# A graph layer's merged stage: items kept in flight over the ends of turns, and a group's last steps moved to the next round

## The chip, the cores and the metric

The kernel runs on one core of a Trainium2 chip. The metric is device time in microseconds, from the median of three runs; smaller is better. A profile of one further execution gives the times of single instructions. TensorE (PE) does the matrix products, VectorE (DVE), ScalarE (ACT) and GpSimd (POOL) the elementwise work, and SyncE (SP) only issues transfers. Each engine has its own stream of instructions, and they wait for one another by semaphores.

## What is computed

Two layers of a graph network on 32768 nodes of 256 features, with 524288 edges. The first layer normalizes each row, applies relu, and runs attention with 8 heads inside blocks of 128 nodes; the second sends messages along the edges in both directions and gates the result:

```python
h = jnp.maximum(_layernorm(x, axis=-1), 0.0)
x = x + _L0_gnn_ref(h, ...)               # attention inside blocks of 128 nodes
h = jnp.maximum(_layernorm(x, axis=-1), 0.0)
# inside the second layer, after a batch norm of h over all nodes:
a_in  = segment_sum(feat_in[src] * iw[:, None], dst, num_segments=N)
a_out = segment_sum(feat_out[dst] * ow[:, None], src, num_segments=N)
# a gate (sigmoid, tanh) of a_in, a_out and h gives the new h
x = x + h
```

The edges come sorted by `dst`, and most of them end at nodes with low numbers.

## The kernel before, in words

The kernel sorts the edges by block of `dst`, builds tables, and then runs a merged stage in which two kinds of work share the engines. After it come the sums over edges and the gates, which the change doesn't touch.

**Groups.** A group is 4 blocks of 128 nodes; there are 64. `project` (layer norm, queries, keys, values) and `attend` (scores, softmax, output, residual sum `x1g`, second layer norm `h1g`, its transpose `h1T`, stores of all three to memory, statistics) each return a table from step number to work. Block `b` of `attend` begins at step `B = 1 + 15 * b`; the last steps of a group reach step 74. Most intermediate values in PSUM have one buffer per name (`mx`, `sc`, `pt`, `mm`).

**Items.** An item is 128 edges with a common block of `dst`. Its steps are: `fetch` (SP loads the block's 128 rows of `h1` from memory into `hb`), `spread_lanes` (TensorE, `bc`, for four items at once), `select` (VectorE: `selT` for four items, the one-hot `oh` for each), `rank` (TensorE: three products into `R`, which counts how many edges of each source block came before), `product` (TensorE: `mp`, the rows of the edges), `place` (VectorE: `jk`, which reads the place out of `R`, and for four items `pi`), `scale` (ScalarE: `msg`) and `scatter` (GpSimd: four indirect transfers for four items). Step `t` of a turn fetches item `t`, ranks and multiplies item `t - 12`, and scales and scatters item `t - 13`.

**Rounds and turns.** A round is 64 items together with one group (`attend` of a group and `project` of the next). There are 68 rounds, in three phases (22, 23, 23). `turns` writes the instructions of a loop body: turns of 4 rounds, whose loop lets engines be in neighbouring quarters of the body (`quarter` marks the borders, and the point 14 steps into a quarter where an engine waits for its work of the quarter before); then turns of 1 round, whose loop ends in a barrier of all engines; then turns of 1 round without groups. Within a turn the items of a round begin while those of the round before are still under way, and the last steps of a group fall among the first steps of the next round. At a turn's end both are worked off: a turn of `n` items has `n + 13` steps.

**The order.** Inside a body it is written out by hand: for each step `t`, first the tables of the next round (`window` at step 10, `derive` from step 24), then the items' steps, then what the groups have put at this step, blocks in order. TensorE, VectorE, ScalarE and SP execute in this order. Steps are counted here from a round's beginning.

**The lead.** A fetched row must have been stored by a group of an earlier round. The number of groups that run alone ahead of the first round (`lead`) is worked out from the tables before the stage begins. With these inputs it is 1: the load of `xg`, one for each `project`, stands at 952.5 us and 1032.9 us before the first round begins at 1073.5 us, and 63 rounds have a group.

Of the kernel before, what the change touches and what calls it, by code (L numbers as in the profile page):

```python
# [499 lines left out]
def gnn_kernel(ctx, tc, x, src, dst, edge_attr, edge_type, w_in_e, w_out_e,  # L500
# [133 lines left out]
    lead = cpool.tile([P, 1], F32, name="lead")  # L634
    UG = 4
# [3 lines left out]
    with tc.tile_pool(name="ld", bufs=1) as lp:  # L639
        need = lp.tile([P, 1], F32, name="need")  # L640
        nc.vector.memset(need, 1.0)
        before = lp.tile([P, 1], F32, name="before")
        nc.vector.memset(before, 0.0)
        for k in range(K):
# [8 lines left out]
            nc.vector.tensor_sub(v, v, r)  # L653
            nc.vector.tensor_scalar(v, v, before[0:CI], None, op0=ALU.subtract)
# [32 lines left out]
    with ExitStack() as c1:  # L687
# [56 lines left out]
        def project(g, qT, kbd):  # L744
# [69 lines left out]
            for b, t in ((0, 47), (2, 67)):  # L814
                ps = {}
                for i in range(2):
                    @at(t + i)
                    def _(b=b, i=i, ps=ps):
                        if i == 0:
                            ps["v"] = a_ps.tile([P, 2, D], F32, name="mx")  # L820
                        for k in range(KC):
                            nc.tensor.matmul(ps["v"][:, i], hT[:, k, (b + i) * P:(b + i + 1) * P], wv[:, k],
                                             start=(k == 0), stop=(k == KC - 1))

                @at(t + 2)
                def _(b=b, ps=ps):
                    nc.scalar.copy(vg[:, b:b + 2, :, 0:DH], ps["v"].rearrange("p b (h d) -> p b h d", d=DH))

            @at(67)
# [5 lines left out]
        def attend(g, qT, kbd, bias=None):  # L835

            todo, at = steps_of()
            for b in range(GB):
                B = 1 + 15 * b
# [73 lines left out]
                if b < GB - 2:  # L913
                    continue

                bs = slice(0, b + 1) if b < GB - 1 else slice(b, b + 1)

                @at(B + 21)
                def _(bs=bs):
                    std(1, bs)  # L920

                @at(B + 22)
                def _(bs=bs):
                    nc.vector.reciprocal(rstd[1][:, bs], rstd[1][:, bs])
                    nc.vector.scalar_tensor_tensor(nmr[:, bs], mv[1][:, bs, 0], -1.0, rstd[1][:, bs],
                                                   op0=ALU.mult, op1=ALU.mult)

                for n, u in enumerate(range(bs.start, bs.stop)):
                    h = {}

                    @at(B + 23 + 3 * n)
                    def _(u=u):
                        nc.scalar.activation(h1g[:, u], x1g[:, u], AF.Relu, bias=nmr[:, u:u + 1], scale=rstd[1][:, u:u + 1])

                    @at(B + 25 + 3 * n)
                    def _(u=u, h=h):
                        h["tp"] = transposed("mx", h1g[:, u])

                    @at(B + 26 + 3 * n)
                    def _(u=u, h=h):  # L940
                        nc.scalar.copy(h1T[:, :, u * P:(u + 1) * P], h["tp"])

            @at(B + 21)
            def _():
                nc.scalar.dma_start(x1_g[g], x1g)

            @at(B + 24)
            def _():
                nc.sync.dma_start(h1_g[g], h1g)

            @at(B + 28)
# [14 lines left out]
        with tc.tile_pool(name="a_k", bufs=1) as kp:  # L966
# [3 lines left out]
            emit(attend(0, qTs[0], kbds[0], bias))  # L970
        lead_n = planned(4 * K, 1, NG)
        with tc.For_i(1, lead_n, 1) as it:
            emit(project(it, qTs[0], kbds[0]))
            emit(attend(it, qTs[0], kbds[0]))
        emit(project(lead_n.with_bounds(min_val=0, max_val=NG - 1), qTs[0], kbds[0]))
# [3 lines left out]
        LEAD = 12  # L979
        fp = c1.enter_context(tc.tile_pool(name="p_f", bufs=1))  # L980
        wp = c1.enter_context(tc.tile_pool(name="p_w", bufs=2))
        sp = c1.enter_context(tc.tile_pool(name="p_s", bufs=2))
        op = c1.enter_context(tc.tile_pool(name="p_o", bufs=7))
        ip = c1.enter_context(tc.tile_pool(name="p_i", bufs=NM))
        hp = c1.enter_context(tc.tile_pool(name="p_h", bufs=14))
# [14 lines left out]
        w0n = fp.tile([CI, 1], F32, name="w0n")  # L1000
        msgs = []
# [5 lines left out]
        def spread(k, lo, hi):  # L1007
# [57 lines left out]
            def begin(c):  # L1065
                for name, t, nxt in (("row", [1, CI], rown), ("dlb", [CI, T1], dlbn), ("ed", [P, 4, CI], edn)):
                    c[name] = wp.tile(t, nxt.dtype, name=f"{name}c")
                    nc.vector.tensor_copy(c[name], nxt)

            def fetch(i, q, c, turn):  # L1070
                if q % 4 == 0:
                    c["at"] = numbers(c["row"][:, q:q + 4], [N - P] * 4)
                hb = turn["hb", i] = hp.tile([P, D], F32, name="hb")
                nc.sync.dma_start(hb, h1_d[ds(c["at"][q % 4], P)])

            def spread_lanes(i, q, c, turn):
                if q % 4 == 0:
                    bc = turn["bc"] = bp.tile([P, 4, T1], F32, name="bc")
                    for j in range(4):
                        nc.tensor.matmul(bc[:, j], cn["pick"][:, q + j], c["dlb"], start=True, stop=True)  # L1080

            def select(i, q, c, turn):
                if q % 4 == 0:
                    sel = turn["sel", i // 4] = sp.tile([P, 4, T1], F32, name="selT")
                    nc.vector.tensor_scalar(sel, turn["bc"], cn["lane"], None, op0=ALU.is_equal)
                oh = turn["oh", i] = op.tile([P, NB], BF16, name="oh")
                nc.vector.tensor_scalar(oh, cn["iota1"], c["ed"][:, 0, q:q + 1], None, op0=ALU.is_equal)  # L1087

            def product(i, q, c, turn):
                if i % 2 == 0:  # L1090
                    turn["mp"] = pp.tile([P, 2, D], F32, name="mp")
                mp = turn["mp", i] = turn["mp"][:, i % 2]
                nc.tensor.matmul(mp, turn["sel", i // 4][:, q % 4], turn.pop(("hb", i)), start=True, stop=True)  # L1093

            def add(what, of, to, turn):
                oh = turn["oh", of]
                nc.tensor.matmul(R[:, to % 2], cn[what], oh, start=False, stop=False, skip_group_check=True)  # L1097

            def rank(i, q, c, turn):

                if i:
                    add("ones_b", i - 1, i, turn)
                if i > 1:
                    add("triu", i - 2, i, turn)
                add("tri", i, i, turn)

            def scale(i, q, c, turn):
                msg = msgs[i // 4 % NM]
                nc.scalar.activation(msg[:, q % 4, 0:D], turn.pop(("mp", i)), AF.Copy, scale=c["ed"][:, 1, q:q + 1])  # L1109
                if q % 4 == 0:  # L1110
                    nc.scalar.copy(msg[:, :, D:FW + 1], c["ed"][:, 1:3, q:q + 4].rearrange("p f j -> p j f"))

            def place(i, q, c, turn):
                if q % 4 == 0:
                    c["pf"] = ip.tile([P, 4], F32, name="pf")
                jk = sp.tile([P, NB], F32, name="jk")
                nc.vector.scalar_tensor_tensor(jk, cn["iota1"], c["ed"][:, 0, q:q + 1], R[:, i % 2], op0=ALU.is_equal,  # L1117
                                               op1=ALU.mult, accum_out=c["pf"][:, q % 4:q % 4 + 1])
                if q % 4 == 3:
                    c["pi"] = ip.tile([P, 4], I32, name="pi")  # L1120
                    nc.vector.tensor_add(c["pi"], c["pf"], c["ed"][:, 3, q - 3:q + 1])

            def scatter(i, q, c, turn):
                if q % 4 == 3:
                    for j in range(4):
                        s = nc.gpsimd.indirect_dma_start(  # L1126
                            out=msg_d[k][:], out_offset=bass.IndirectOffsetOnAxis(ap=c["pi"][:, j:j + 1], axis=0),
                            in_=msgs[i // 4 % NM][:, j], in_offset=None, bounds_check=hi - lo - 1, oob_is_err=False)
# [3 lines left out]

            steps = ((0, fetch), (LEAD - 4, spread_lanes), (LEAD - 2, select), (LEAD, rank), (LEAD, product), (LEAD, place),
                     (LEAD + 1, scale), (LEAD + 1, scatter))

            def turns(begin_at, end, nr, groups):


                several = nr > 1
                with tc.For_i(begin_at, end, nr, **({"iteration_sync": "staggered"} if several else {"hint_engines": ENGINES})) as it:  # L1140
                    cs, turn, todo, n = [], {}, {}, nr * CI
                    last = steps[-1][0]
                    with tc.manual_schedule(engines=IN_ORDER):
                        for t in range(n + last):
                            if several:
                                quarter(t, [0] + [i * CI + 3 for i in range(1, nr)], last + 1)
                            r, q = divmod(t, CI)
                            if r < nr:
                                after = ds((it + (r + 1)).with_bounds(min_val=0, max_val=NC1[k]), 1)
                                if q == 0:  # L1150
                                    cs.append({})
                                    begin(cs[r])
                                    if groups is not None:
                                        now, then = r % 2, (r + 1) % 2
                                        g = lambda i: (it + groups + (r + i)).with_bounds(min_val=0, max_val=NG - 1)
                                        for work in (attend(g(0), qTs[now], kbds[now]), project(g(1), qTs[then], kbds[then])):
                                            for u, fs in work.items():
                                                assert u < CI + last
                                                todo.setdefault(t + u, []).extend(fs)
# [6 lines left out]
                            for lag, step in steps:  # L1166
                                i = t - lag
# [285 lines left out]
```

## Time and profile before

| | us |
|---|---|
| runs (three) | 19862.4, 19876.65 (median), 19916.4 |
| the profiled execution, its own time | 17164.17 |
| its span, first to last instruction | 17162.3 |
| busy in the span: PE, DVE, ACT, POOL | 14133.3, 10222.2, 6748.4, 9315.0 |
| mean granted TensorE clock | 0.924 |
| merged stage, from the first round to the end of the last | about 1073 to 8910 |

The profiled execution took 2712 us less than the median of the runs; durations below are from it. A group line of the profile gives source line, engine, operation, output and inputs, count, busy time, mean duration in ns, and after the bar the idle time of the engine just before these instructions with what ended it (`<-PE R L1097` is: TensorE's writing of `R` at line 1097). A line of a stretch gives its borders, its length, the busy time and count of each engine, the granted clock of TensorE, the share of the DMA engines and GB/s. A line of the timeline gives start, duration, engine, source line, operation, and in brackets the idle time before it. A TensorE duration contains the pipeline's depth: back to back, the 128x256 products into `R` start 0.107 us apart and those into `mp` 0.215 us apart.

### The profile page before, as it was taken

How to read it: one execution, taken by the hardware profiler on the slowest of the kernel's cores; microseconds unless marked ns; L12 is line 12 of the kernel's file. 1: busy time of each engine (PE TensorE's matmuls, PEld its weight loads, DVE VectorE, ACT ScalarE, POOL GpSimd, SP SyncE). 2: the span in 40 equal slices, each digit the busy share in tenths (PEclk: the TensorE clock that was granted, in tenths of full speed). 3: DMA queues.
4: the chain of work that ended last, by engine and by line, in shares of the span. 5: the costliest groups of instructions: out<-in, count | busy, mean ns of one | idle time of the engine just before them, and what ended most of it. 6: DMA issues, size and time to landing. Idle time of an engine off the chain costs nothing. (4 is left out here: it accounts for less than half of the span.)

```text
span 17162.3 us, 294157 instructions
## 1 busy us (share of the span) xinstructions
PE 14133.3 (82%) x71780; PEld 10281.3 (60%) x71780; DVE 10222.2 (60%) x33823; ACT 6748.4 (39%) x17011; POOL 9315.0 (54%) x9309
## 2 busy tenths in 40 slices
PE   2068888888888878888769999888888888898988
PEld 1046666656666656666548778777777777633433
DVE  8757777767777767777655555555555555422222
ACT  0035555545555445555424444444444444300000
POOL 0035555555555555555567777776767666522221
PEclk6579999989999989999889999999999999999999
DMA  1035555545555535555558888788878888833332
GB/s 64 10 95 171 170 173 167 167 144 167 169 168 165 163 123 168 171 169 166 163 156 244 241 243 245 233 240 233 239 231 236 229 234 238 186 128 108 107 116 92
DMA packets 1830396, 2975.33 MB, mean 173 GB/s; under 512 B 299498, under 2 KB 1289287, under 8 KB 1828438
## 3 DMA queue, kind: packets, MB, share of 16 engines
q1 hardware_dynamic: 1203190, 1584.46, 30.6%
q0 software_dynamic: 430768, 1160.40, 22.8%
q10 hardware_dynamic: 194864, 212.95, 4.0%
q8 instruction: 564, 9.24, 0.2%
q14 instruction: 1010, 8.27, 0.2%
HBM read 2124.16 MB, written 1248.64 MB: 197 GB/s over the span
## 5 line engine op out<-in xcount | busy, mean ns | idle before, releaser
L1126 POOL DMA_INDIRECT msg_d<-msg,pi x4352 | 4298.7, 988 | 3034.7 <-ACT msg L1109 798.9
L1259 POOL DMA_INDIRECT rows<-h_d,ixc x3584 | 3405.3, 950 | 1362.2 <-PE ps_i L1273 327.7
L1109 ACT ACTIVATE msg<-mp,edc 128x256 f32<-128x256 f32 x4352 | 2005.2, 476 | 3497.6 <-PE mp L1093 3181.6
L1117 DVE SCALAR_TENSOR_TENSOR jk<-iota,edc,R 128x256 f32<-128x256 bf16 x4352 | 2077.8, 477 | 1742.6 <-PE R L1097 1709.0
L1294 ACT ACTIVATE selo<-lane_row,sl 128x128 f32<-128x128 f32 x5040 | 1662.3, 391 | 3383.3 <-DVE sl L1291 2751.6
L1273 PE MATMUL ps_i<-rows,sel 128*128 128x257 f32 x8960 | 2502.0, 398 | 334.8 <-DVE acc L1277 244.3
L1301 PE MATMUL ps_o<-m,selo 128*128 128x257 f32 x10080 | 2566.0, 392 | 203.4 <-ACT selo L1295 201.0
L1093 PE MATMUL mp<-hb,selT 128*128 128x256 f32 x8704 | 2716.4, 395 | 3.5 <-DMA hb<-h_d 3.5
L1301 PEld LDWEIGHTS ps_o<-m,selo 128*128 128x128 f32 x10080 | 1866.7, 194 | 513.5 <-ACT selo L1295 179.2
L1273 PEld LDWEIGHTS ps_i<-rows,sel 128*128 128x128 f32 x8960 | 1562.9, 198 | 587.3 <-DVE acc L1277 364.3
L1097 PE MATMUL R<-oh,ones_b 128*128 128x256 bf16 x4352 | 1217.1, 280 | 796.4 <-DVE jk L1117 672.3
L1266 DVE TENSOR_SCALAR sel<-lane_row,ed 128x128 f32<-128x128 f32 x4480 | 1393.0, 358 | 621.4 <-PE idle L1274 570.2
L1093 PEld LDWEIGHTS mp<-hb,selT 128*128 128x128 f32 x8704 | 1371.6, 199 | 69.9 <-DMA hb<-h_d 5.7
L1087 DVE TENSOR_SCALAR oh<-iota,edc 128x256 bf16<-128x256 bf16 x4352 | 1381.9, 318 | 6.5 <-issue 2.5
L1305 DVE SCALAR_TENSOR_TENSOR acc<-acc,blk,ps_o 128x257 f32<-128x257 f32 x1680 | 804.7, 479 | 852.3 <-PE ps_o L1301 705.9
L1097 PEld LDWEIGHTS <-triu 128*128 128x128 bf16 x4352 | 428.1, 98 | 1474.5 <-issue 1422.1
L1097 PE MATMUL R<-oh,tri 128*128 128x256 bf16 x4352 | 1219.3, 280 | 0.0
L1097 PE MATMUL R<-oh,triu 128*128 128x256 bf16 x4352 | 1206.5, 278 | 0.0
L1277 DVE SCALAR_TENSOR_TENSOR acc<-acc,blk,ps_i 128x257 f32<-128x257 f32 x2240 | 1068.6, 477 | 204.1 <-PE ps_i L1273 77.8
L1291 DVE TENSOR_SCALAR sl<-m,blk 128x3 f32<-128x3 f32 x1680 | 426.6, 254 | 1082.6 <-DMA m<-msg_d 1074.5
L1259 POOL DMA_INDIRECT rows<-h_d,ixh x896 | 850.8, 950 | 371.0 <-issue 136.3
L1295 ACT ACTIVATE selo<-selo,one 128x384 f32<-128x384 f32 x1680 | 1031.4, 614 | 52.2
(362 smaller groups left out, 20945.1 us busy)
## 6 DMA issues: line engine op xcount, KB each, us to landing
m<-msg_d SPq DMA_DIRECT2D x1680, 396.0 KB
hb<-h_d SPq DMA_DIRECT2D x4352, 128.0 KB, 2.2
sin_d<-acc SPq DMA_DIRECT2D x2240, 128.5 KB
sout_d<-acc SPq DMA_DIRECT2D x1680, 128.5 KB
msg_d<-msg,pi POOLq DMA_INDIRECT x4352
more<-sout_d ACTq DMA_DIRECT2D x128, 514.0 KB
rows<-h_d,ixc POOLq DMA_INDIRECT x3584
xg<-in_x SPq DMA_DIRECT2D x65, 512.0 KB
```

Source lines behind the costliest of these rows:

```text
L1087: nc.vector.tensor_scalar(oh, cn["iota1"], c["ed"][:, 0, q:q + 1], None, op0=ALU.is_equal)
L1093: nc.tensor.matmul(mp, turn["sel", i // 4][:, q % 4], turn.pop(("hb", i)), start=True, stop=True)
L1097: nc.tensor.matmul(R[:, to % 2], cn[what], oh, start=False, stop=False, skip_group_check=True)
L1109: nc.scalar.activation(msg[:, q % 4, 0:D], turn.pop(("mp", i)), AF.Copy, scale=c["ed"][:, 1, q:q + 1])
L1117: nc.vector.scalar_tensor_tensor(jk, cn["iota1"], c["ed"][:, 0, q:q + 1], R[:, i % 2], op0=ALU.is_equal, op1=ALU.mult, accum_out=c["pf"][: ...
L1126: s = nc.gpsimd.indirect_dma_start(out=msg_d[k][:], out_offset=bass.IndirectOffsetOnAxis(ap=c["pi"][:, j:j + 1], axis=0), in_=msgs[i // 4 ...
L1259: nc.gpsimd.indirect_dma_start(out=rows[(2 * i + r) % NR][:, 0:D], out_offset=None, in_=h1_d[:], in_offset=bass.IndirectOffsetOnAxis(ap=(i ...
L1266: nc.vector.tensor_scalar(sel[:, r], cn["lane_row"], c["ed"][:, 0, r, i:i + 1], c["ed"][:, 1, r, i:i + 1], op0=ALU.is_equal, op1=ALU.mult)
L1273: nc.tensor.matmul(ps, sel[:, r], rows[(2 * i + r) % NR], start=(r == 0), stop=(r == 1))
L1277: nc.vector.scalar_tensor_tensor(acc[0][i % NA], acc[0][(i - 1) % NA], c["blk"][:, 0, i:i + 1], c.pop(("t_ps", i)), op0=ALU.mult, op1=ALU.add)
L1294: nc.scalar.activation(sel[:, r], cn["lane_row"], AF.Abs, bias=sl[:, r:r + 1])
L1301: nc.tensor.matmul(ps, sel[:, r], m[:, r, 0:FW], start=(r == 0), stop=(r == T3 // P - 1))
```

## The change

Items now live across the end of a turn. The loop body has `n + 1` steps; step `t` fetches item `t + 12`, spreads lanes of `t + 4`, selects for `t + 2`, ranks, multiplies and places item `t`, and scales and scatters `t - 1`. The last steps of a turn thus begin the next turn's items. What such items need is kept in tiles of fixed numbers (16 `hb`, 8 `oh`, 2 `selT`, and two sets of the round's tables, `rowc`, `dlbc`, `edc`, filled by `begin` at step 46 of the round before). Ahead of each phase the first 12 steps are issued once outside the loops, and a turn of one round ends with a copy of the second set to the first.

A group has to fit into the 64 steps of its round: blocks of `attend` begin every 14 steps, not 15; the second half of the values (`vg`) moves from step 67 to 60, the sum `xb` from 67 to 63, and `h1g` and `h1T` of the first three blocks follow each other every 2 steps, not 3. The rest (norm of the last block, its transposes, the three stores, the statistics) becomes `store`, which runs in the first 8 steps of the next round, or alone after the last round of a phase that has groups. The store of `h1` is issued by ScalarE, not by SP. Because a round's first items are fetched before the last group's store, the first 24 items of each round (`EARLY`) need one group more when the lead is worked out. The wait inside a quarter moves from 14 steps to 40.

```diff
+    EARLY = 24
+        early = lp.tile([CI, 1], F32, name="early")
+        nc.vector.tensor_scalar(early, cn["lane"][0:CI], float(EARLY), None, op0=ALU.is_lt)
             nc.vector.tensor_sub(v, v, r)
+            nc.vector.tensor_scalar(v, v, early, None, op0=ALU.add)
...
-            for b, t in ((0, 47), (2, 67)):
+            for b, t in ((0, 47), (2, 60)):
...
-            @at(67)
+            @at(63)
             def _():
                 nc.gpsimd.tensor_add(xb, xg, bo_b[:, None, :].to_broadcast([P, GB, D]))
...
-                B = 1 + 15 * b
+                B = 1 + 14 * b
...
+            norm(at, slice(0, GB - 1), B - 14 + 21)
+            return todo
+
+        def norm(at, bs, t):
+            @at(t)
+            def _():
+                std(1, bs)
+            @at(t + 1)
+            def _():
+                nc.vector.reciprocal(rstd[1][:, bs], rstd[1][:, bs])
+                nc.vector.scalar_tensor_tensor(nmr[:, bs], mv[1][:, bs, 0], -1.0, rstd[1][:, bs],
+                                               op0=ALU.mult, op1=ALU.mult)
+            for n, u in enumerate(range(bs.start, bs.stop)):
+                h = {}
+                @at(t + 2 + 2 * n)
+                def _(u=u):
+                    nc.scalar.activation(h1g[:, u], x1g[:, u], AF.Relu, bias=nmr[:, u:u + 1], scale=rstd[1][:, u:u + 1])
+                @at(t + 4 + 2 * n)
+                def _(u=u, h=h):
+                    h["tp"] = transposed("mx", h1g[:, u])
+                @at(t + 5 + 2 * n)
+                def _(u=u, h=h):
+                    nc.scalar.copy(h1T[:, :, u * P:(u + 1) * P], h["tp"])
+
+        def store(g):
+            todo, at = steps_of()
+            norm(at, slice(GB - 1, GB), 1)
+            @at(2)
             def _():
                 nc.scalar.dma_start(x1_g[g], x1g)
-            @at(B + 24)
-                nc.sync.dma_start(h1_g[g], h1g)
-            @at(B + 28)
+            @at(4)
+            def _():
+                nc.scalar.dma_start(h1_g[g], h1g)
+            @at(8)
             def _():
                 nc.scalar.dma_start(h1T_g[g], h1T)
...
-            steps = ((0, fetch), (LEAD - 4, spread_lanes), (LEAD - 2, select), (LEAD, rank), (LEAD, product), (LEAD, place),
-                     (LEAD + 1, scale), (LEAD + 1, scatter))
+            steps = ((12, fetch), (4, spread_lanes), (2, select), (0, rank), (0, product), (0, place), (-1, scale), (-1, scatter))
...
-                        for t in range(n + last):
+                        for t in range(n + 1):
                             if several:
-                                quarter(t, [0] + [i * CI + 3 for i in range(1, nr)], last + 1)
+                                quarter(t, [0] + [i * CI + 3 for i in range(1, nr)], 40)
...
+                                    for work in (store(g(-1)), attend(g(0), qTs[now], kbds[now]),
+                                                 project(g(1), qTs[then], kbds[then])):
...
+                                if q == 46:
+                                    begin((r + 1) % 2)
+                            items(t, turn, 0 if t < n else n - 1, n + 64 if t < n else n)
...
+                        if nr % 2:
+                            for of in (rowc, dlbc, edc):
+                                nc.vector.tensor_copy(of[0], of[1])
...
             for _ in derive(slice(0, 1)):
                 pass
+            begin(0)
+            for t in ohs[NO - 2:]:
+                nc.vector.memset(t, 0.0)
+            with tc.manual_schedule(engines=IN_ORDER):
+                turn = {}
+                for t in range(-steps[0][0], 0):
+                    items(t, turn, 0, CI)
...
             turns(many, both, 1, before)
+            emit(store((both + before - 1).with_bounds(min_val=0, max_val=NG - 1)))
             turns(both, planned(2 * K + k, 1, NC1[k]), 1, None)
```

## The prediction

> **What bounds the kernel.** I read the page first (groups of instructions), then busy time by stretches, one for each round of the merged stage, and then the order of single instructions. The groups name the three operations that every item has on TensorE and VectorE (busy, mean ns, idle before and who ended it):
>
> ```profile
> L1117 DVE SCALAR_TENSOR_TENSOR jk<-iota,edc,R 128x256 f32<-128x256 bf16 x4352 | 2077.8, 477 | 1742.6 <-PE R L1097 1709.0
> L1093 PE MATMUL mp<-hb,selT 128*128 128x256 f32 x8704 | 2716.4, 395 | 3.5 <-DMA hb<-h_d 3.5
> L1097 PE MATMUL R<-oh,ones_b 128*128 128x256 bf16 x4352 | 1217.1, 280 | 796.4 <-DVE jk L1117 672.3
> ```
>
> TensorE waits for VectorE (`R` for `jk`) and VectorE for TensorE (`jk` for `R`): one chain goes to and fro. The stretches below run from one copy of the row table (`rowc`, VectorE, once a round) to the next; columns are length, busy time of TensorE, weight loads, VectorE, ScalarE, GpSimd, granted clock, DMA:
>
> ```profile
> 4093.40:4195.20 101.80, 87.49 (x491) 60.73 (x491) 69.16 (x251) 48.19 (x128) 52.66 (x54) 0.90 0.50 159
> 4195.20:4307.60 112.40, 98.27 (x574) 70.33 (x572) 83.12 (x301) 58.54 (x152) 66.31 (x67) 0.95 0.54 170
> 4420.20:4551.10 130.90, 112.91 (x656) 80.38 (x654) 97.85 (x349) 69.11 (x176) 80.00 (x79) 0.96 0.53 171
> 5933.00:6064.30 131.30, 101.11 (x570) 70.77 (x570) 87.21 (x300) 58.26 (x152) 67.85 (x66) 0.88 0.45 146
> 8615.10:8713.10 98.00, 66.31 (x388) 41.91 (x388) 60.44 (x242) 29.00 (x82) 63.99 (x65) 0.88 0.53 169
> ```
>
> First, inner and last round of a turn of four; a turn of one; a round without a group. Turn ends cost little: 101.8 + 112.4 + 112.6 + 130.9 = 457.7 is only 8 over four inner rounds. A round of its own costs 19 more. Another inner round, at full clock throughout:
>
> ```profile
> 2204.50:2311.90 107.40, 93.73 (x574) 66.79 (x572) 83.52 (x301) 58.56 (x152) 66.42 (x67) 1.00 0.56 180
> ```
>
> What fills these 107.4? The order on VectorE at steps 10 and 11 of this round:
>
> ```profile
> 2223.64 0.47 DVE L1117 SCALAR_TENSOR_TENSOR jk<-iota,edc,R 128x256 f32<-128x256 bf16 x1
> ...
> 2224.03 0.68 DVE L956 BATCH_NORM_STATS2 st<-h1T 128x6 f32<-128x512 f32 x1
> ...
> 2224.83 0.69 DVE L956 BATCH_NORM_STATS2 st<-h1T 128x6 f32<-128x512 f32 x1
> ...
> 2225.63 0.42 DVE L732 BATCH_NORM_STATS2 st<-xg 128x6 f32<-128x256 f32 x1
> ...
> 2226.88 0.47 DVE L1117 SCALAR_TENSOR_TENSOR jk<-iota,edc,R 128x256 f32<-128x256 bf16 x1
> ```
>
> and on TensorE:
>
> ```profile
> 2224.16 0.27 PE L1097 MATMUL R<-oh,ones_b 128*128 128x256 bf16 x1 [1.42 <-DVE jk L1117]
> ...
> 2227.42 0.27 PE L1097 MATMUL R<-oh,ones_b 128*128 128x256 bf16 x1 [1.79 <-DVE jk L1117]
> ```
>
> The group's vector work of a step stands ahead of the next item's `jk`, and TensorE may not rank the item after that before it. So a step lasts as long as the longer of two: TensorE 0.75 (three `R` at 0.107, two `mp` at 0.215) plus the group's matmuls, and 0.3 each fourth step for the lanes (`bc`); VectorE 0.06 + the group's work of the step before + 0.20 `oh` + 0.48 `jk`, and 0.67 more each fourth step for `selT`. Here 0.06 + 2.68 + 0.20 + 0.48 = 3.4, measured 3.26. There is no slack of several items between the engines: it matters which group work falls in which step.
>
> The clock follows from it. Of a later inner round:
>
> ```profile
> 4215.80:4219.20 3.40, 1.61 (x13) 1.08 (x12) 3.08 (x13) 2.89 (x5) 0.76 (x1) 1.00 0.88 279
> 4219.20:4229.40 10.20, 10.05 (x43) 8.13 (x42) 4.67 (x21) 2.05 (x6) 5.10 (x6) 0.50 0.35 112
> ```
>
> The same two waits, falling into one 3.4 us stretch, are followed by 10.2 us at half clock: 5.1 us, the difference of 112.5 and 107.4. [...]
>
> [...] an index add (`pi`) that takes 0.16 elsewhere took 2.42 at 2211.4, beside the 2.37 us `xb` add.
>
> **The change, part by part.**
>
> *Ends of the turns of four.* What goes there: TensorE's wait of 4.36 us for `selT` (at 4562.99), behind VectorE's 3.75 us for the load of `xg`, while no item was begun. In the three phases the 5, 5 and 4 such turns take 2282.9, 2299.2 and 1815.1 us, 103 over 56 × 112.4. Remaining: the last turn of each phase must still drain (13.2 from last `mp` to the loop's end, and about 4 to begin a loop: 17 × 3 = 51), and 12 items are now begun ahead of each phase (12 fetches at about 0.65 with their register loads, barrier: 13 × 3 = 39). Gain 13.
>
> *Rounds of their own.* Seven now, 914 us without the starts of phases. Each loses its fill (first `mp` 12.6 us after the start, of which some 4 did group work) and keeps the drain, since scatters trail: 122.4, six of them, 734. Gain 180, one round of which moves to the next line.
>
> *Lead.* The first 24 items of a round now need one group more; round 0 needs group 0, so lead goes from 1 to 2, 62 rounds have groups, and six (now five) have none. A group alone takes 80.4 (loads of `xg` at 952.5 and 1032.9), with the loop 88. Rounds without a group are bound by 64 scatters at 1.29 (0.99 + 0.30): 95 each, 570 for 490. Loss 168.
>
> *Stores.* Three outside the loops, about 9 each (table load 1.3, activation, two transposes, copy, two 0.69 statistics): loss 27. Inside, the `h1` store leaves SP's queue, where it held SP some 6 us a round behind the landing of fetches, for ScalarE's, between the `x1` and `h1T` stores. ScalarE gets 0.4 of issue and a wait for fetches up to item 16. Queued behind it is `scale`, on which TensorE's `mp` banks wait after four items. That fetch can go out when item 0's product is done, three items earlier, and lands in 2.2: hidden; if not, up to 3 a round, 190. SP's next fetches wait for the store, 12 items ahead of use: hidden.
>
> *Copies* (`rowc`, `dlbc`, `edc`, 0.63) move within the round: nothing. Begun items use the same engines in the same relative order: nothing. The sync point 40 steps into a stage replaces one at 14, where no engine waits long in this trace: nothing.
>
> *The group packed into 64 steps.* Blocks stand 14 apart, not 15; V's second half at 60, `xb` at 63 (the blocked VectorE instruction stays, at another place). At 15, block b's `x1g` add and statistics (0.42 + 0.43 + 0.18, 1.05 with gaps) came one step before block b+1's `nm` and `PT` (0.68 each). At 14 all fall in one step: 21, 35, 49, 2.41 us together. Steps 22 and 50 have a `selT` too: 0.06 + 2.41 + 0.67 + 0.20 + 0.48 = 3.8; step 36, 3.2. There TensorE has 0.75 to 1.05 of work. The step before is its heavy one: `y` and `sc` now fall in one step (20, 34, 48, up to 2.9). I added up 64 steps by the rule, with the rows' durations:
>
> | steps | before, trace | before, rule | after, rule |
> |---|---|---|---|
> | 0–19 | 34.2 | 35.3 | 35.1 |
> | 20–23 | 7.3 | 7.8 | 8.6 |
> | 24–37 | 26.1 | 26.5 | 26.7 |
> | 38–47 | 16.3 | 16.1 | 18.8 |
> | 48–53 | 9.7 | 9.8 | 11.7 |
> | 54–63 | 13.7 | 14.9 | 15.4 |
> | sum | 107.4 | 110.4 | 116.2 |
>
> The rule is 3 high; the difference, 5.8, I take as 5 (2 to 7). Clock: TensorE idles 3.0, 2.2 and 3.0 us at one stretch in steps 22, 36 and 50, more than the two waits above in one piece, so I expect 3 half-clock stretches a round (1 to 4) for 0.9, each worth 4, since light steps follow: +8 (0 to +12). Together +13 at full count; the rule overstates stalls (21 us of them, 13.6 in the trace), so I take +10: 62 × 10 = 620.
>
> *Sum:* −13 − 180 + 168 + 27 + 620 = +622. On the profiled execution (17164.2, 2 outside its span) that is 17786, +3.6%. The timed median, 19876.65, is 2712 longer and the trace can't say why; if slower TensorE stretches are the reason, steps are longer too. I carry over +664, between 622 and 3.6% of the median (720): 20540.
>
> **Rivals.**
> *Only the packing costs, the clock doesn't:* 62 × 5 = 310, about 20190. For it: light neighbours are already common. Against it: one 3.4 us stretch of waits already halves the clock in most rounds.
> *The round keeps its 112.4, and turn ends give all they seem to hold:* −103, −128 (seven singles at 112.4), +88 lead, −14 (a 112 us round becomes one of 98) = −157, 19720, faster. It decides where packing adds under 157/62 = 2.5 us a round. For it: VectorE is busy 83 of 107, so there is room; against it: the 3.26 us step above.
> *Everything in full:* +18 a round, 1116, about 20990.
> *The change does nothing:* drains take the fills' place and the round grows by under 1 us.
>
> **How the numbers follow.** Packing with clock 0.55, packing alone 0.22, in full 0.06: slower 0.83. Turn ends win 0.12; nothing 0.05, within 0.3% (60 us, about what this measurement can tell). The likeliest case alone spans 20270 to 20900. 8 in 10: from 19850, which leaves out the faster case, to 21150, the full case with some of the unexplained 2712.
>
> **What would show it.** Inner rounds of about 122 instead of 112; a granted clock near 0.87 in them, three half-clock stretches locked to the round; waits of `R` for `jk` of 2 to 3 us at steps 22, 36, 50, and `x1g`, `nm`, `PT`, `selT` in one row on VectorE ahead of them; no gap at turn ends; three loads of `xg` ahead of the first round, six rounds without a group. Wrong: inner rounds under 114.

## The result, and the profile after

| | median us | runs |
|---|---|---|
| before | 19894.64 | 6 (19862.4 to 19916.4) |
| after | 19790.53 | 6 (19734.51 to 19803.92) |

The ratio is 0.9945, with a 95% interval of 0.9929 to 0.996: 104 us faster. The forecast was 20540 and slower, with a range from 19850 up; it was wrong.

One thing has to be known to read what follows: the same program takes one of two times, about 17170 and 17420 us for the kernel before on two of the chips used here, about 20040 and 19800 on two others. I call these the short and the long condition. Each of these chips was used for one series of runs only, so whether the chip decides or something else that differed between the series isn't shown. The six runs above are long ones. The profile of before that the prediction was worked out from (17164) was a short one, and the profile of after (19778.6) is long. These two profiles must not be laid side by side; the experiments supply pairs that can be.

The page of after, the groups that answer to those shown of before:

```profile
L1123 DVE SCALAR_TENSOR_TENSOR jk<-iota,edc,R 128x256 f32<-128x256 bf16 x4352 | 2076.8, 477 | 3260.0 <-PE R L1111 1625.7
L1106 PE MATMUL mp<-hb,selT 128*128 128x256 f32 x8704 | 2944.2, 424 | 0.0
L1111 PE MATMUL R<-oh,ones_b 128*128 128x256 bf16 x4352 | 1284.1, 295 | 1923.8 <-DVE jk L1123 1118.0
```

VectorE's `jk` takes what it took (477 ns in both), so it has not become slower in itself; TensorE's means are longer, and its clock is lower (0.889 in the mean, for 0.924). The idle time has grown, and half of what `jk` waits (3260.0) is not put down to `R` any more (1625.7).

Stretches of after, one inner round each, from the first `mp` of one round to that of the next (length, busy time and count of TensorE, weight loads, VectorE, ScalarE, GpSimd, then granted clock, DMA share, GB/s):

```profile
4256.30:4388.88 132.58, 102.98 (x574) 71.42 (x573) 82.48 (x300) 59.08 (x152) 66.41 (x66) 0.91 0.45 145
4388.88:4521.13 132.25, 105.49 (x574) 72.84 (x573) 83.13 (x300) 58.69 (x152) 66.37 (x66) 0.90 0.45 145
4654.47:4792.97 138.50, 105.82 (x575) 73.04 (x573) 82.51 (x299) 59.66 (x153) 66.55 (x66) 0.88 0.43 138
```

132 to 138 us, with the same work on every engine as in the 112 us round of before; TensorE alone is busy for longer, 103 to 106 us where that round has 98. And the row on VectorE at step 50 of such a round is just the one that the prediction named:

```profile
4621.15 0.48 DVE L1123 SCALAR_TENSOR_TENSOR jk<-iota,edc,R 128x256 f32<-128x256 bf16 x1 [2.88 <-PE R L1111]
...
4621.56 0.42 DVE L915 TENSOR_TENSOR x1g<-mm,xb 128x256 f32<-128x256 f32 x1
4622.01 0.43 DVE L737 BATCH_NORM_STATS2 st<-x1g 128x6 f32<-128x256 f32 x1
...
4622.57 0.66 DVE L881 COPY PT<-pt 128x512 f32<-128x512 f32 x1
4623.14 0.68 DVE L861 TENSOR_REDUCE nm<-sc 128x4 f32<-128x512 f32 x1
4623.74 0.74 DVE L1099 TENSOR_SCALAR selT<-bc,lane 128x512 f32<-128x512 f32 x1
4624.40 0.28 DVE L1100 TENSOR_SCALAR oh<-iota,edc 128x256 bf16<-128x256 bf16 x1
4624.59 0.47 DVE L1123 SCALAR_TENSOR_TENSOR jk<-iota,edc,R 128x256 f32<-128x256 bf16 x1
```

TensorE waits beside it:

```profile
4625.13 0.27 PE L1111 MATMUL R<-oh,ones_b 128*128 128x256 bf16 x1 [2.52 <-DVE jk L1123]
```

So the packing's pile-up is there (3.44 us for the step), the rounds are longer than forecast, and the kernel is faster all the same. Two questions follow: does the packing cost what I worked out, and why doesn't the timed run pay for it?

### The profile page after: what moved, and what is told of

It reads as the page before. It is cut to its first block, busy times and chain, and to the rows that moved or that the text cites. A ratio compares the mean times of both kernels' runs of the same rounds, so it can differ in the third digit from the quotient of the medians.

```text
span 19778.6 us, 294973 instructions
## 1 busy us (share of the span) xinstructions
PE 14937.9 (76%) x71798; PEld 10700.7 (54%) x71798; DVE 10152.4 (51%) x33904; ACT 6778.9 (34%) x17038; POOL 9312.2 (47%) x9309
## 5 line engine op out<-in xcount | busy, mean ns | idle before, releaser
L1123 DVE SCALAR_TENSOR_TENSOR jk<-iota,edc,R 128x256 f32<-128x256 bf16 x4352 | 2076.8, 477 | 3260.0 <-PE R L1111 1625.7
L1289 PE MATMUL ps_i<-rows,sel 128*128 128x257 f32 x8960 | 2620.1, 413 | 776.9 <-DVE acc L1293 384.2
L1317 PE MATMUL ps_o<-m,selo 128*128 128x257 f32 x10080 | 2748.7, 413 | 596.5 <-ACT selo L1311 281.0
L1106 PE MATMUL mp<-hb,selT 128*128 128x256 f32 x8704 | 2944.2, 424 | 0.0
L1111 PE MATMUL R<-oh,ones_b 128*128 128x256 bf16 x4352 | 1284.1, 295 | 1923.8 <-DVE jk L1123 1118.0
L1317 PEld LDWEIGHTS ps_o<-m,selo 128*128 128x128 f32 x10080 | 1969.9, 205 | 993.8 <-issue 292.9
L1289 PEld LDWEIGHTS ps_i<-rows,sel 128*128 128x128 f32 x8960 | 1626.8, 205 | 1069.7 <-DVE acc L1293 445.9
L1106 PEld LDWEIGHTS mp<-hb,selT 128*128 128x128 f32 x8704 | 1503.6, 216 | 94.8
L1111 PE MATMUL R<-oh,tri 128*128 128x256 bf16 x4352 | 1298.8, 298 | 0.0
L1111 PE MATMUL R<-oh,triu 128*128 128x256 bf16 x4352 | 1298.1, 298 | 0.0
## 6 DMA issues: line engine op xcount, KB each, us to landing
hb<-h_d SPq DMA_DIRECT2D x4388, 128.0 KB
```

The source lines that it names most:

```text
L1106: nc.tensor.matmul(mp, sels[q // 4 % 2][:, q % 4], hbs[q % NH], start=True, stop=True)
L1111: nc.tensor.matmul(R[:, q % 2], cn[what], ohs[of % NO], start=False, stop=False, skip_group_check=True)
L1123: nc.vector.scalar_tensor_tensor(jk, cn["iota1"], edc[z][:, 0, q:q + 1], R[:, q % 2], op0=ALU.is_equal, op1=ALU.mult, accum_out=turn["pf"] ...
L1289: nc.tensor.matmul(ps, sel[:, r], rows[(2 * i + r) % NR], start=(r == 0), stop=(r == 1))
L1317: nc.tensor.matmul(ps, sel[:, r], m[:, r, 0:FW], start=(r == 0), stop=(r == T3 // P - 1))
```

## The experiments

My theory at first: the packing costs 5 to 13 us a round, and the ends of turns, the lead and the stores come out at about nothing; the profile of after hides it because the two profiles are of different conditions. The first rival: packing costs nothing, and the turn ends give more than I priced. A second rival came up later: packing and the move over the ends interlock, so that one is harmless only with the other.

**The kernel before, unchanged**, to see which condition a run is in and whether profiling changes the time.

> The kernel before, unchanged, with a new profile. The changed kernel's profile shows inner rounds of 132.7 us and 19780 us in all; the profile of the kernel before showed 112.4 and 17164, though its runs take 19895. If that profile was of an execution without the stalls that the runs have, this one shows 19800 to 19950, inner rounds near 133, and idle time of engines that no other engine's work ends. If rounds really became 20 us longer by the change (packing), it shows 112 to 113 again while its own time is near 17164.

Measured: 17170.68 in the profiled run, clock 0.924, and 17173.38 for the median of 19 runs beside it. A profiled execution takes what a timed one takes. So the 2712 us that the prediction could not explain are not an effect of profiling.

**The packing alone, on the kernel before:**

```diff
-            for b, t in ((0, 47), (2, 67)):
+            for b, t in ((0, 47), (2, 60)):
...
-            @at(67)
+            @at(63)
...
-                B = 1 + 15 * b
+                B = 1 + 14 * b
...
-                    @at(B + 23 + 3 * n)
+                    @at(B + 23 + 2 * n)
...
-                    @at(B + 25 + 3 * n)
+                    @at(B + 25 + 2 * n)
...
-                    @at(B + 26 + 3 * n)
+                    @at(B + 26 + 2 * n)
```

> The kernel before with the packing alone: blocks 14 steps apart, V at 60, xb at 63, h1 of the first three blocks every 2 steps; items, turn ends and the place of the last steps as before. Packing theory (step sums of the prediction, 5 to 10 us a round): 310 to 620 us slower, ratio 1.015 to 1.03. Rival (the stalls that runs have hide which step the group's work is in): within 60 us, ratio 0.997 to 1.003.

Measured, short condition: 17673.17 against 17173.38, ratio 1.0288 (1.0268 to 1.0308). That is 500 us, 8 for each of 63 rounds with a group. The first rival falls for this condition.

**The changed kernel with the placement of before:** items in flight over the ends as in after, but blocks 15 steps apart and transposes every 3 steps as before; what then doesn't fit into 64 steps (the last block's output product and sum, the second half of the values, `xb`) goes to the next round's first 10 steps with the stores.

```diff
-                B = 1 + 14 * b
+                B = 1 + 15 * b
...
-            norm(at, slice(0, GB - 1), B - 14 + 21)
...
+            norm(at, slice(0, GB - 1), B - 15 + 21)
...
-                @at(t + 2 + 2 * n)
+                @at(t + 2 + 3 * n)
...
-            norm(at, slice(GB - 1, GB), 1)
+            ends(at, GB - 1, {"oT": oTl}, 1)
+            norm(at, slice(GB - 1, GB), 3)
...
-            for work in (store(g(-1)), attend(g(0), qTs[now], kbds[now]),
+            for work in (store(g(-1)), late(), attend(g(0), qTs[now], kbds[now]),
```

> The changed kernel, items in flight over turn ends, but with the group's work at the steps where it was before: blocks 15 apart, what lies beyond step 63 (last block's output product and sum, V's second half, xb, norm, stores) in the next round's first 10 steps. Packing theory: faster than the changed kernel by 310 to 620 us, ratio to before 0.963 to 0.98. Rival: like the changed kernel, ratio 0.991 to 0.998.

Measured, short condition: 17147.34 against 17173.38, ratio 0.9982 (0.9974 to 0.9991), 26 us faster. What the change is worth with the placement loosened is this little; the prediction's sum for all but the packing was +2. Both ratios expected, 0.963 to 0.98 and 0.991 to 0.998, missed, since they took the changed kernel's place to be that of the long runs, 0.9945. Where the changed kernel was timed in the short condition (below), the loose form is 378 us faster than it, within the 310 to 620 of the packing theory.

**The changed kernel with one step of the pile-up moved:** the sum `x1g` and its statistics of the first three blocks one step later, away from `nm` and `PT`.

```diff
-                @at(B + 20)
+                @at(B + 20 + (b < GB - 1))
```

> The changed kernel with one thing moved: the sum x1g and its statistics of blocks 0 to 2 one step later (21 steps after the block's begin, not 20), so that they don't fall in one step with nm and PT of the next block. Packing theory with the pile-up on VectorE as its cause: steps 22, 36 and 50 shorten from 3.4 to about 2.6 and the clock is halved less often: 2 to 5 us a round, 120 to 300 us faster than the changed kernel, ratio to before 0.98 to 0.989. If the pile-up is no cause: within 60 us of the changed kernel, ratio 0.991 to 0.998.

Measured, short condition: 17306.92 against 17173.38, ratio 1.0081 (1.0056 to 1.0107). The ratio expected was again worked out from the long runs, so only the difference from the changed kernel can be compared. Beside the ratio of the changed kernel in the short condition, 1.0196 on another chip (below), it is some 200 us less, 3.2 for each of 62 rounds, within the 2 to 5 expected. The traces agree: from one `jk` to the next, the steps with the pile-up last 3.44, 2.98 and 3.44 us in the changed kernel and 2.46, 2.00 and 2.46 here (medians of the inner rounds 23 to 40), the steps after them grow by 0.5 to 0.8 us, and the mean inner round is 116.0 instead of 119.0 us. The time at half clock falls as well, from 12.1 to 8.3 us a round. So this pile-up, with the half clock that goes with it, makes up about half of what the packing costs in the changed kernel; the other half isn't taken apart.

**The changed kernel, unchanged, and the kernel before with a lead of two groups** (`need` set to 2.0, not 1.0, ahead of the search for the lead):

> The changed kernel, unchanged. If the kernel before takes about 17170 beside it: packing theory, the parts add up: 500 for packing alone, less 26 for the rest (items in flight with the old placement were 26 faster), 17650, ratio 1.02 to 1.03, and inner rounds of 118 to 121. If the change is worth what the runs of the result showed whatever the chip: ratio 0.993 to 0.996, 17080. If the kernel before takes about 19895 beside it: ratio 0.993 to 0.996 again.

> The kernel before with one group more in the lead: two groups run alone, 62 rounds have a group, six have none. Prediction's terms: 88 for the group alone, less 14 to 30 for a round without a group in place of one of its own with a group: 55 to 75 us slower than before, ratio 1.003 to 1.0045. Rival (the group's work merely moves, its time is saved in the round it leaves): within 20 us, ratio 0.999 to 1.001.

Measured, long condition: after 19996.63 against 20041.68, ratio 0.9978 (0.9969 to 0.9988), 45 us faster; 0.993 to 0.996 was expected. Lead 2: 20116.27, ratio 1.0041 (1.0026 to 1.0056), 75 us. The prediction's arithmetic for it (88 for the group alone, less 14 for a round that loses its group) gives 74. This run also gives a profile of before, apart from the lead, in the long condition.

So the packing costs 500 us in one condition, and the kernel that contains it is 45 us faster in the other. The next four ran side by side on one chip, in the short condition:

> The changed kernel as it is. Theory A (the packing costs about 8 us a round, and this is covered only where the rounds are already stretched to about 132 us by idle time that the profile puts down to nothing): beside a before of about 17170 us it takes 1.5 to 2.8 per cent longer (pack alone cost 500, the looser placement of the same change gained 26), beside a before of about 20040 us it takes 0.2 to 0.6 per cent less. Theory B (packing and the move over the ends interlock, so that the packed loop is harmless once no turn ends in between): 0.995 to 1.002 beside either.

> The packing alone, on the kernel before. Beside a before of about 17170 us: 1.029 again, both theories. Beside a before of about 20040 us: theory A 1.000 to 1.012, since an inner round there has about 20 us of idle time that no engine ends, in which 8 us of packing find room; a theory in which the packing costs the same everywhere: 1.025.

> The items in flight over the ends of turns with the placement of before. Beside a before of about 17170 us: 0.998 again. Beside a before of about 20040 us: theory A 0.980 to 0.995, since the last round of a group of four costs 16 us more than an inner one there (8 where before takes 17170) and none of that is left in this kernel; that it gains nothing beyond the 0.998 of the other condition would say that the end of a turn is no dearer there.

> The kernel before, for a profile on the same chip as the three others. Rounds inside a group of four: 112 us where it takes about 17170 us, about 130 us where it takes about 20040 us, and the last of four 120 or about 147.

| beside a before of 17423.91 us | us | ratio (95%) |
|---|---|---|
| after | 17763.06 | 1.0196 (1.0179 to 1.0213) |
| packing alone | 17909.49 | 1.0282 (1.0265 to 1.03) |
| in flight, placement of before | 17385.29 | 0.9978 (0.9971 to 0.9986) |

The changed kernel is 2% slower here, and in the direction that was forecast. The rival of interlocking parts falls, since its 0.995 to 1.002 was to hold beside either. The difference of after and its loose form, 17763 − 17385 = 378 us, is what the packing costs in it, 6.1 for each of 62 rounds (but for what the loose form adds to the first 10 steps of a round). The groups of the kernel before and of after, same chip, say where (page, after the bar the idle time ahead of these instructions):

```profile
L1097 PE MATMUL R<-oh,ones_b 128*128 128x256 bf16 x4352 | 1218.8, 280 | 798.0 <-DVE jk L1117 674.1
```

```profile
L1111 PE MATMUL R<-oh,ones_b 128*128 128x256 bf16 x4352 | 1238.2, 285 | 1226.3 <-DVE jk L1123 1131.0
```

TensorE waits 428 us more ahead of `R`, and 457 more of it for `jk`: the wait that the prediction named. One inner round of before and two of after in these runs:

```profile
3896.01:4008.89 112.88, 98.53 (x574) 70.25 (x573) 82.61 (x300) 58.67 (x152) 66.31 (x66) 0.95 0.54 169
```

```profile
4070.61:4190.00 119.39, 99.16 (x575) 69.41 (x573) 82.80 (x300) 58.80 (x152) 66.51 (x66) 0.96 0.50 161
4430.50:4548.53 118.03, 100.16 (x574) 69.82 (x573) 83.27 (x300) 58.76 (x152) 66.40 (x66) 0.94 0.51 164
```

Five to seven us longer at the same clock, 0.95 against 0.94 to 0.96. Over the whole round the clock of the changed kernel costs no more than before's (12.1 us at half clock a round for 12.8, in the table below).

Last, packing alone and the loose form again, in the long condition:

> The packing alone, for the condition in which before takes about 20000 us. Theory A (the packing's 8 us a round are covered by the idle time of the stretched rounds): 1.000 to 1.012 there. A theory in which the packing costs the same everywhere: 1.025. Beside a before of 17200 to 17450 us: 1.028 for the third time.

> The items in flight over the ends of turns with the placement of before, for the condition in which before takes about 20000 us. Theory A: 0.980 to 0.995 there, since the last round of four is 16 us dearer than an inner one and this kernel has no such last round; 0.998 as in the other condition would say that the end of a turn gives no more there. Beside a before of 17200 to 17450 us: 0.998 for the third time.

Measured beside a before of 19802.49: packing alone 19737.07, ratio 0.9968 (0.9958 to 0.9978); loose form 19728.59, ratio 0.9963 (0.9953 to 0.9972). The edit that costs 500 us in the short condition costs nothing here. This is the main finding, and it isn't exactly what I had expected: I wrote 1.000 to 1.012 for the packing, and it came out 65 us below; and 0.980 to 0.995 for the loose form, which came out above, at −74. Of that miss some 75 us are the second group of lead, which I had left out of the expectation though the run with a lead of two had measured it.

The same rounds in all conditions (means from first `mp` to first `mp`, rounds 23 to 40, all of them in turns of four in the kernels that have turn ends; one execution each; rows with one letter were taken on one chip, and of the row without a letter the chip isn't recorded):

| kernel | condition, chip | inner of four | last of four | half clock, us a round |
|---|---|---|---|---|
| before | short, A | 112.6 | 120.5 | 12.8 |
| packing alone | short, A | 120.5 | 128.0 | 18.7 |
| packing alone | short, B | 119.3 | 127.9 | 16.4 |
| in flight, loose | short, A | 112.7 | 112.8 | 10.5 |
| after | short, A | 119.0 | 120.1 | 12.1 |
| after, one step moved | short, B | 116.0 | 116.0 | 8.3 |
| before, lead 2 | long, C | 132.0 | 146.9 | 33.9 |
| after | long, C | 134.9 | 135.0 | 27.7 |
| packing alone | long, D | 130.8 | 144.6 | 27.2 |
| in flight, loose | long, D | 131.7 | 131.4 | 31.0 |
| after (result's profile) | long | 133.5 | 132.6 | 27.4 |

(Half clock is a mean over rounds 23 to 41.) In the short condition the placement of the group decides the inner round: 113 or 119 to 120. In the long one it is 131 to 135 whichever placement is used, and the last round of four, where turns end, stands 14 to 15 above, not 8. On chip C, the only one with profiles of both placements and the same lead, the changed kernel's inner rounds are 2.9 us longer than before's, with single rounds scattering by 2 to 3 us; so some of the packing's cost may remain there. On chip D the packed inner round is 0.9 us shorter than the loose one.

**What stretches the rounds.** Not a longer `jk`, as the means show (477 to 478 ns). Step 20 of the same round of after, in the two conditions. Short, TensorE and then VectorE:

```profile
4226.17 0.27 PE L1111 MATMUL R<-oh,tri 128*128 128x256 bf16 x1
```

```profile
4226.48 0.48 DVE L1123 SCALAR_TENSOR_TENSOR jk<-iota,edc,R 128x256 f32<-128x256 bf16 x1
```

Long, the same two instructions:

```profile
4557.84 0.27 PE L1111 MATMUL R<-oh,tri 128*128 128x256 bf16 x1
```

```profile
4557.82 0.27 DVE L1100 TENSOR_SCALAR oh<-iota,edc 128x256 bf16<-128x256 bf16 x1
4562.91 0.48 DVE L1123 SCALAR_TENSOR_TENSOR jk<-iota,edc,R 128x256 f32<-128x256 bf16 x1 [4.83 <-remote]
```

Here `jk` waits for one semaphore of TensorE alone. In the short run it starts 0.31 us after the start of the product that it needs; in the long run 5.07 after it. "Remote" is what the profile writes where no instruction is found to have raised the semaphore just then. The trace's own record of that semaphore shows updates at 4558.54, 4558.59, and then 4560.02, 4560.73, 4561.45, 4561.48, 4562.16, 4562.85 and 4562.89: TensorE's matmuls of 4557.3 to 4560.5, done by their records, are reported late and some 0.7 us apart. I then set every recorded update of TensorE's semaphores against the end of the last matmul that raises that semaphore:

| after | updates recorded, of matmuls that make one | over 0.3 us late |
|---|---|---|
| merged stage, short | 26462 of 26771 | 0 |
| merged stage, long | 20802 of 26771 | 2485 |
| sums over edges, short | 13567 of 13604 | 2 |
| sums over edges, long | 10069 of 13604 | 2364 |
| gates, short | 1050 of 1042 | 8 |
| gates, long | 1050 of 1042 | 8 |

The kernel before with lead 2 gives 3790 late of 20602 in the long condition, and before 0 of 26542 in the short one. The lateness is TensorE's alone, but the gaps in the record are not: in the merged stage of after, of the semaphores that almost only VectorE or only ScalarE raises, the long trace has 9037 of 14144 and 5143 of 8836 updates, where the short one has nearly all, and of these none and 4 came 0.3 to 20 us after an instruction's end. So the counts of late ones are counts of those that were recorded. The stages with late updates are those that are longer: merged 8094 against 9131, sums 6338 against 7330, and the rest, from the last sum on, 2134 against 2132. So in the long condition word of a finished TensorE instruction often arrives late at the engines that wait for it: 2485 of the 20802 updates recorded in the merged stage came over 0.3 us late. The lower clock is the smaller part of the longer rounds: TensorE is busy 103 to 106 us in the long rounds of after shown above, 99 to 100 in the short ones, while a round is some 14 us longer. (In the gates the count is above the matmuls', since weight loads raise a semaphore of TensorE a few times too. The end of a TensorE instruction is modelled in these records, so the product itself may have been late; the engine that waits sees no difference.) Why it is so on those chips isn't settled: a scatter lands about 2.3 us after its issue in both conditions, so slower scatters aren't what one sees, and I made no run that changes the number of updates. That lateness hides the packing is argued, from two facts. The pile-up steps last the same in both conditions (3.44, 2.98 and 3.44 us in after, medians of the inner rounds), so it is the late part that is smaller in a packed round (long less short, inner rounds: 133.5 − 119.0 = 14.5 and 134.9 − 119.0 = 15.9 in after, 130.8 − 120.5 = 10.3 with packing alone, but 132.0 − 112.6 = 19.4 in before and 131.7 − 112.7 = 19.0 in the loose form; these are differences between chips). And VectorE's idle time ahead of `jk` hardly grows. On chip C, before with lead 2 and after:

```profile
L1117 DVE SCALAR_TENSOR_TENSOR jk<-iota,edc,R 128x256 f32<-128x256 bf16 x4352 | 2078.8, 478 | 3352.8 <-PE R L1097 1501.8
```

```profile
L1123 DVE SCALAR_TENSOR_TENSOR jk<-iota,edc,R 128x256 f32<-128x256 bf16 x4352 | 2076.5, 477 | 3391.3 <-PE R L1111 1509.4
```

That is 39 us more, where the same idle time grows by 411 us in the short condition (1757.2 to 2168.6 on chip A). No run shows directly that the lateness hides the packing.

## Why the prediction was wrong, by its steps

- **What bounds the kernel** (one chain between `R` and `jk`): right in the condition of the profile read. In the condition of the timed runs something more adds some 19 us to an inner round of before, and that profile, taken in the other condition, has no trace of it (0 late updates).
- **Packing, by the step rule** (+5, between 2 and 7): right for the changed kernel in the short condition. 119.0 − 112.7 = 6.3 a round, 378 us in the difference of the times; half of it goes with the pile-up named, as the run with one step moved shows. Packing alone cost 7 to 8 a round. The table of steps is near: the round of after at 4430.5 in the short condition has 33.8, 9.3, 26.8, 18.7, 14.1 and 15.3, together 118.0, where the rule gave 35.1, 8.6, 26.7, 18.8, 11.7 and 15.4, 116.2; its neighbours take 119.4 to 120.3. That the sums agree so well is in part luck: the rule is for full clock and was 3 high on before, and the measured rounds contain half clock. The waits of `R` for `jk` of 2 to 3 us are there, 2.52 in step 50 in both conditions.
- **Clock** (+8 a round, together +10): mis-sized. There are indeed 3 half-clock stretches a round (2.9, where before has 1.0), but they last 3.4 or 6.8 us where before has mostly 10.2 or 13.7, and the total is 12.1 us for 12.8. (Packing alone did raise the total, to 18.7.) The granted clock of inner rounds is 0.93 to 0.96, not 0.87. I gave each new stretch nearly the length of the old one. What makes a stretch set in was not shown: of the two waits that I put into one stretch of before, 4215.80 to 4219.20, only the second lies in it (1.79 us, to 4218.40), the first (1.41 us) ended at 4215.15; and the round at 2204.5 has two of the same lengths, 1.42 and 1.79, and is at full clock throughout. Without this step the sum is about +310, which was the prediction's first rival; the short condition measured +339 (17763.06 − 17423.91).
- **Ends, rounds of their own, lead, stores** (−13 − 180 + 168 + 27 = +2): near in sum, −26 and −39 measured with the loose form, but by luck, since its parts were off: the last round of four lost 7.7 us (about 108 in 14 turns, where I allowed 13 with the fills of phases), and rounds of their own lost 4 to 6 (131.0, 130.5 and 134.5 became 125.8, 126.7 and 129.0), where 914 for seven becoming 734 for six meant 8 each. A round without a group was put at 95, which 64 scatters at 1.29 don't give (83); it took 97 to 98. The lead came out as priced, 75 for 74, though measured in the long condition and priced in the short one; in the short condition the first `mp` of after is at 1159.94, 68 after that of before (1091.98).
- **"I carry over +664"**: this is the step that failed, and it decided the sign. I noted a difference of 2712 us between the profiled and the timed runs, called it unexplained, guessed that steps are longer by a ratio there, and scaled the whole effect with it. But the time that is added there is mostly idle time of engines, and most of the waits of the packing don't come on top of it. In the long condition the packing alone is worth −65, where it is worth +486 and +500 in the short one, and the whole change is small: −45 on one chip, −104 in the runs of the result. Why the waits don't add up there is argued above and not shown.
- **The faster rival** (19720; decides where packing adds under 2.5 us a round) came nearest, by luck. Its point is not clearly met: on chip C inner rounds go from 132.0 to 134.9. Its reason, that VectorE has room, fails in the short condition, where packing costs 6 us and more a round, and the round of the timed condition is not the 112.4 that it starts from. How the 45 to 104 us divide is open: on chip D the loose form and the packing alone give 74 and 65, and these don't add up to what the changed kernel gained on other chips. Nor is it known why packing alone is faster than before there.

## What to carry to other kernels

Before an effect is carried from a profile to timed runs, the profile's own time has to agree with them; where it is 14% off (17164 to 19877), a sum made on it holds for the condition of that profile, and may not even have the right sign in the other. If two conditions exist, a change that loses in one can win in the other: the loose form is the one that was faster than before in both (0.9982 and 0.9978, 0.9963), while the change as made is 1.0196 in one and 0.9945 to 0.9978 in the other. Adding up an order of instructions step by step predicted what packing adds to a loop within about 1 us in 120 (5.8 against 6.3) in the condition of its profile; what such a sum can't give is the clock, whose stretches have to be counted in time and not in number: 2.9 of them a round came to 12.1 us, where 1.0 had come to 12.8.

## What the runs showed of the hardware

*Rounds that keep step with the clock.* With no turn ends and the short condition, the loose form repeats: each of the rounds 23 to 40 has one half-clock stretch of 10.2 us. Columns as in the stretches above:

```profile
3856.00:3866.24 10.24, 10.22 (x44) 8.01 (x42) 4.73 (x19) 2.05 (x6) 5.01 (x6) 0.50 0.50 150
3866.24:3968.65 102.41, 88.06 (x531) 62.08 (x530) 78.06 (x281) 56.61 (x145) 61.33 (x61) 1.00 0.54 171
3968.65:3978.89 10.24, 10.24 (x44) 8.04 (x43) 4.73 (x19) 2.15 (x7) 4.95 (x5) 0.50 0.49 158
```

10.24 us at half clock and 102.41 at full, 112.65 together, are 3 and 30 times 3.413 us. The same unit is in the trace of before: of its 200 half-clock stretches all but the last, which ends with the trace, are whole multiples of 3.413 us (72 of one, 34 each of two and three), and the changes of its clock lie within 0.03 us of one grid of that spacing. In the loose form, from round 24 to 41, the half clock sets in 23.1 to 23.5 us after the round begins, so a round begins at nearly the same place in the grid each time. Whether the half clock sets the length of the round was not shown.

*One program, two times.* 17170 and 17420 us on two chips, 19800 and 20040 on two others, with `jk` at 477 to 478 ns in all, and late updates of TensorE's semaphores in the longer ones alone. In the merged stage of after, the long trace has no record of 22% of TensorE's updates, 36% of VectorE's and 42% of ScalarE's, by the counts above.
